# A second Strassen step shared by pairs of text units, and part of the adapter's transposes moved from TensorE to VectorE

## The chip, the cores and the metric

One core of one Trainium2 chip runs the kernel; the other cores are idle. The metric is the device time of one execution in microseconds, as the median of several runs. TensorE is called PE below, its weight loads PEld, VectorE DVE, ScalarE ACT, GpSimd POOL and SyncE SP.

## What is computed

Cross-attention with an adapter, for x of 2 x 2048 x 640 and a context of 2 x 128 x 384, all in float32, with 8 heads of 80:

```python
query = hidden_states @ Wq
hs = _mha(query, enc @ Wk, enc @ Wv)            # 124 text tokens
ca_q1 = einsum('btc,th->bch', ca, Wq_ca)        # 4 adapter tokens -> 384 rows
ca_hs1 = _mha(ca_q1[:, indices], residual, residual)
ca_hs2 = _mha(ca_hs1 @ Wq, ca @ Wk_ca, ca @ Wv_ca)
out = (hs + ca_hs2) @ Wout + b_out + residual
```

`indices` picks 2048 rows out of 384, so the adapter has 384 distinct rows per batch.

## The kernel before

**Work.** The 4096 rows of x are 16 *text units* m of 256 rows (two tiles i of 128). For each, the kernel makes queries (PSUM tiles `pq`), scores (`sc`), a softmax on ACT, DVE and POOL, sends the probabilities through HBM to turn them (`kept`, back as `pT`), multiplies them with the values (`ph`) into the hidden tile `hs`, and multiplies that with Wout (`po`). Beside it runs the *adapter* of each batch b: a first pass of scores (`s1`), whose row maxima DVE takes (`mx`), a second pass (`s2`) whose exponentials ACT takes (`ea`), and a contraction with the rows of y (`acc`). Its row maxima are spread into a tile `mt`, turned by PE transposes into `pm`, subtracted from the operand `ca0` and split into the pair of operands `cop` (`halves_of`, one ACT cast and one DVE instruction over 2 x 384 columns). The result `acc` is copied to `accs`, turned by three PE transposes into `pt_acc`, divided (`prod`), and leads to the 384 adapter rows (`second`). POOL gathers those rows onto each output tile by an indirect DMA (`add_second`) before the tile is stored.

**The product with Wout** (`text_out_fast`, L2392). hs (256 x 640) times Wout (640 x 640) goes by one Strassen step on the first 512 of K: seven products of 128 rows, 256 of K and 320 columns instead of eight, and the last 128 of K, the *fifth*, is multiplied plainly. The sums s1 to s4 of hs are made by DVE or POOL, those of Wout once (`wout_sums`). The seven products stand in four *chains* (L2438), each in one PSUM bank:

```python
            (((a[0][0], w[0][0], None), one_h, ((0, 0),)), ((s2, t2, None), [("hs", m, "s2")], ((1, 0),)),
             ((s1, t1, None), [("hs", m, "s1")], ((0, 1),)), ((None, None, (1, 1)), end_h, ((1, 1),))),
            (((s3, t3, None), [("hs", m, "s3")], ((1, 1),)), ((a[1][1], t4, (1, 0)), both_h + end_h, ((1, 0),))),
            (((a[0][1], w[1][0], (0, 0)), both_h + end_h, ((0, 0),)),),
            (((s4, w[1][1], (0, 1)), [("hs", m, "s4")] + end_h, ((0, 1),)),),
```

Each step is a product added onto what the bank holds; the pair at its end is the quarter (i, u) of the output rows to which DVE then adds the bank (`add`). The next step of the chain waits for that add. One product is written by `by_columns` (L402): four matmuls, one for each 32 columns of the weights, which run side by side in the array; each float32 matmul is two instructions in the trace.

**The order.** The kernel is written as tasks that yield operations (`Do`) with what they wait for and what room they need. A table `TURNS` (L80), worked out ahead, gives every operation its place and engine; `run` (L351) issues by it, and `pin` keeps that order. Where an operation may go to several engines, the table says to which. Text units come in the order 0, 4, 2, 1, 5, 13, 6, 7, 15, 3, 12, 9, 14, 10, 11, 8 (unit 15's product with Wout comes last). Helpers record the instructions, so most rows have L396 (`matmul`), L405 (`by_columns`), L410 (`transpose`), L427 (DVE, ACT and POOL) or L447 (DMA).

Of the kernel before, what the change touches and what calls it, by code (L numbers as in the profile page):

```python
# [8 lines left out]
F32 = mybir.dt.float32  # L9
# [5 lines left out]
P = 128  # L15
# [50 lines left out]
class Desk:  # L66
# [2525 lines left out]
```

## Time and profile before

| | |
|---|---|
| median of 3 runs | 573.56 us (573.53 to 573.89) |
| the profiled execution | 572.92 us |
| its span | 570.9 us |
| PE, PEld busy | 563.0 us, 309.6 us |
| DVE, ACT, POOL busy | 394.5 us, 287.1 us, 160.1 us |
| DMA | 113.21 MB, mean 198 GB/s |
| granted clock of PE | 1.000 |

A row of the timeline or of a group names the line of the helper, the engine, the operation, and the tiles written and read; `128*32 128x320` is a matmul that uses 128 rows and 32 columns of the array and streams 320 columns. Behind the bar stand the busy time of the group in us, the mean of one in ns, and the idle time of the engine just before with what ended it. An arrow in a waits row goes from the engine that waited to the one that released it.

### The profile page before, as it was taken

What the parts mean: (1) busy time and instruction counts of PE and PEld (TensorE: products, weight loads), DVE (VectorE), ACT (ScalarE), POOL (GpSimd) and SP (SyncE); (2) the same over time, 40 slices, a digit from 0 to 9 for tenths busy, and PEclk for the clock granted to TensorE, in tenths of its full rate; (3) what the DMA queues carried; (4) which work ended last, traced back from release to release, by engine and by line L of the source; (5) the groups of instructions that cost most, each with busy time, mean ns of one, the idle gap of its engine ahead of it and who ended that gap; (6) DMA issues with size and microseconds to landing.
All of it is one profiled execution on the core that took longest, in us unless ns stands there. A gap on an engine that the chain in (4) does not pass through costs nothing.

```text
span 570.9 us, 18875 instructions
## 1 busy us (share of the span) xinstructions
PE 563.0 (99%) x8069; PEld 309.6 (54%) x8069; DVE 394.5 (69%) x659; ACT 287.1 (50%) x806; POOL 160.1 (28%) x213
## 2 busy tenths in 40 slices
PE   8999999999999999999999999999999999999997
PEld 8885335455555455466554554555555554455553
DVE  4366999999998577458999999998332213544443
ACT  2021355645566899899885754534554664100000
POOL 9102041114440731100004350531203053045152
PEclk9999999999999999999999999999999999999999
DMA  8998476965968977446646979987476587788888
GB/s 245 219 239 141 125 160 154 175 179 133 209 214 153 221 177 214 149 123 201 228 153 201 328 187 316 224 241 228 94 248 131 167 185 243 251 217 212 255 182 209
DMA packets 145691, 113.21 MB, mean 198 GB/s; under 512 B 82548, under 2 KB 116980, under 8 KB 145608
## 3 DMA queue, kind: packets, MB, share of 16 engines
q1 hardware_dynamic: 137144, 95.43, 59.9%
q0 software_dynamic: 5632, 10.69, 11.6%
q10 hardware_dynamic: 2832, 5.90, 3.0%
q8 instruction: 63, 1.03, 0.8%
q14 instruction: 20, 0.16, 0.1%
HBM read 71.60 MB, written 40.39 MB: 196 GB/s over the span
## 4 chain that ended last, share of the span: by engine, by line
PE 93%; ACT 3%; DVE 3%; DMA 1%; issue 0%; SPq 0%; ACTq 0%
PE po L405 28%; PE pq L405 24%; PE sc L396 8%; PE acc L396 7%; PE ph L396 7%; PE s L396 7%; PE pq L396 4%; PE pyz L396 2%; ACT ea L427 2%; PE pv L396 1%; DVE mx L427 1%; PE pk L396 1%; DMA xz<-in_x_dram 1%; ACT p L427 1%; PE pt_wq L410 1%; PE pw L396 0%
## 5 line engine op out<-in xcount | busy, mean ns | idle before, releaser
L427 ACT ACTIVATE p<-sc,m 128x124 f32<-128x124 f32 x256 | 90.4, 382 | 43.0 <-DVE m L427 38.0
L427 DVE TENSOR_REDUCE mx<-s 128x4 f32<-128x2048 f32 x48 | 109.0, 2270 | 1.9 <-PE s L396 1.9
L427 ACT ACTIVATE ea<-s 128x2048 f32<-128x2048 f32 x48 | 90.5, 1886 | 30.9 <-PE s L396 30.5
L405 PE MATMUL po<-wout_sums,hs 128*32 128x320 f32 x1024 | 78.4, 434 | 0.1
L405 PE MATMUL po<-wout_sb,hs 128*32 128x320 f32 x928 | 72.3, 433 | 0.0
L427 POOL TENSOR_TENSOR p<-p,r 128x992 f32<-128x992 f32 x17 | 31.4, 1849 | 130.9 <-DVE r L427 130.9
L405 PE MATMUL pq<-xt,wq_sb 128*32 128x256 f32 (+1 forms) x928 | 66.4, 418 | 0.0
L427 DVE TENSOR_TENSOR last_rows<-last_rows,po 128x320 f32<-128x320 f32 x60 | 28.0, 480 | 44.0 <-PE po L405 43.8
L427 ACT ACTIVATION_READ_ACCUMULATOR p<-sc,m 128x1 f32 x256 | 57.2, 223 | 0.0
L427 DVE TENSOR_TENSOR x_more<-x_more,po 128x320 f32<-128x320 f32 x68 | 32.3, 480 | 34.2 <-PE po L405 33.7
L405 PEld LDWEIGHTS po<-wout_sums,hs 128*32 128x32 f32 x1024 | 33.4, 110 | 32.7 <-issue 2.7
L427 DVE TENSOR_REDUCE m<-sc 128x4 f32<-128x496 f32 x64 | 40.7, 661 | 14.1 <-PE sc L396 14.0
L396 PE MATMUL acc<-ea,y_sb 128*32 128x384 f32 (+2 forms) x768 | 50.2, 382 | 0.2 <-ACT ea L427 0.2
L396 PE MATMUL ph<-pT,vpad 128*32 128x256 f32 x768 | 47.7, 381 | 0.0
L405 PEld LDWEIGHTS po<-wout_sb,hs 128*32 128x32 f32 x928 | 30.1, 110 | 28.3 <-issue 1.6
L2351 POOL DMA_INDIRECT x_more<-o,query x17 | 26.6, 1564 | 65.2 <-DVE x_more L427 31.1
L405 PEld LDWEIGHTS pq<-xt,wq_sb 128*32 128x32 f32 x928 | 27.7, 110 | 28.0 <-issue 13.5
L427 ACT COPY hs<-ph 128x512 f32<-128x512 f32 (+1 forms) x25 | 13.4, 552 | 57.7 <-PE ph L396 57.7
L427 DVE STREAM_TRANSPOSE eb<-p 128x1024 f32<-128x1024 f32 x32 | 39.4, 1232 | 1.2 <-POOL p L427 1.1
L396 PEld LDWEIGHTS sc<-kmain,q 64*128 64x128 f32 x512 | 31.8, 187 | 12.6 <-issue 5.8
L427 POOL TENSOR_TENSOR hs<-hs 128x256 f32<-128x256 f32 x31 | 28.9, 1020 | 33.7 <-ACT hs L427 25.4
L396 PE MATMUL sc<-kmain,q 64*128 64x124 f32 x512 | 38.0, 285 | 0.0
(219 smaller groups left out, 834.4 us busy)
## 6 DMA issues: line engine op xcount, KB each, us to landing
kept<-eb SPq DMA_DIRECT2D x32, 512.0 KB, 3.5
pT<-kept SPq DMA_DIRECT2D x16, 1024.0 KB, 8.0
landing<-away SPq DMA_DIRECT2D x15, 512.0 KB, 4.8
xi<-in_x_dram SPq DMA_DIRECT2D x56, 128.0 KB, 4.2
x_more<-in_x_dram SPq DMA_DIRECT2D x17, 320.0 KB, 5.0
last_rows<-in_x_dram SPq DMA_DIRECT2D x15, 320.0 KB, 4.8
y<-yt SPq DMA_DIRECT2D x16, 256.0 KB, 3.9
y_sb<-y SPq DMA_DIRECT2D x32, 128.0 KB, 4.0
```

Of the source, the lines that this page charges most:

```text
L396: self.pin(self.nc.tensor.matmul(out, lhsT, rhs, **kw))
L405: self.pin(self.nc.tensor.matmul(out[j : j + 32], lhsT[:, j : j + 32], rhs, **kw))
L410: self.pin(self.nc.tensor.transpose(out, in_, ident))
L427: self.pin(getattr(engine, what)(*args, **kw))
L2351: desk.pin(nc.gpsimd.indirect_dma_start(out=t, out_offset=None, in_=o2_of[b], in_offset=bass.IndirectOffsetOnAxis(ap=query[:, st : st + 1] ...
```

## The change

**Pairs.** Five pairs of text units, (6, 7), (3, 12), (9, 14), (10, 11) and (8, 15), share a second Strassen step. Of the seven products of a unit three, a01 x w10, s4 x w11 and a11 x t4, have weights that both units of a pair use. Stacked, the two units' operands make a product of 256 rows, 256 of K and 320 columns, which is done by seven block products of 128 x 128 x 160 instead of eight (`joint`, PSUM tiles `pi`). The fifths of these three are done in halves of 160 columns beside them. What the inner step needs are sums of Wout quarters, made once (`take_inner`, in the rooms of the softmax tiles `p` and a new `inner_w`), and eight sums per pair (`inner_x0` and others, two buffers), on DVE or POOL. Chain 1 of a paired unit keeps only s3 x t3, which is now added to two quarters. The last unit's s3 x t3 is cut into two halves of columns, and its stores for tile 0 into pieces of 160 columns.

**The adapter.** Of the maxima, half 0 is still turned on the PE; half 1 is turned by 16 DVE transposes of 32 partitions by 3 x 32 (`turned_blocks`), as is `accs` of batch 1, half 0. Each half of `cop` is split on its own, and the scores of half 0 no longer wait for half 1.

**The order.** `turns` puts the pairs behind units 0, 4, 2, 1, 5 and 13, `TURNS` is worked out anew, and the set of first transposes of Wq waits only for its rows.

On the PE, the products of unit 7 that this change moves into the pair, before (`po_7_2` is a01 x w10, `po_7_3` is s4 x w11; `s2` and `acc` are the adapter's):

```order
L405 MATMUL po_7_2_6012<-wout_sb_100,hs_2_5064 32x320 x8
L405 MATMUL po_7_2_6012<-wout_sb_100,wout_sums_4129 32x320 x4
L396 MATMUL s2_1_1_6_6027<-cop_153,zop_1_2_3731 128x384 x4
L396 MATMUL s2_1_1_6_6027<-cop_153,zop_1_2_3731 128x128 x4
L405 MATMUL po_7_3_6037<-wout_sb_100,hs_2_5064 32x320 x8
L405 MATMUL po_7_3_6037<-wout_sb_100,wout_sums_4129 32x320 x4
```

Now the same kind of work on the PE, in pair 1 (units 3 and 12); `pi_1_1_0` is pair 1, product 1, chain 0, and each row of four is one block product:

```order
L434 MATMUL pi_1_1_0_6495<-wout_sb_100,hs_1_4221 32x160 x4
L434 MATMUL pi_1_2_0_6379<-wout_sb_100,hs_0_4133 32x160 x4
L434 MATMUL pi_1_1_2_6507<-wout_sb_100,hs_1_4221 32x160 x4
L434 MATMUL pi_1_1_2_6507<-wout_sb_100,wout_sums_4132 32x160 x4
L434 MATMUL pi_1_2_1_6472<-inner_w_5470,hs_0_4133 32x160 x4
L434 MATMUL pi_1_2_1_6472<-wout_sb_100,hs_0_4133 32x160 x4
L434 MATMUL pi_1_1_0_6495<-p_1_826,inner_x2_5648 32x160 x4
L434 MATMUL pi_1_1_3_6535<-wout_sb_100,inner_x2_5648 32x160 x4
L434 MATMUL pi_1_1_3_6535<-wout_sb_100,wout_sums_4132 32x160 x4
L434 MATMUL pi_1_1_0_6495<-p_1_826,inner_x2_5648 32x160 x4
```

A product of two chunks of 320 columns has become single block products of 160, and between two steps of one chain (the last and the fourth row from the end) stand two others.

On DVE, the adds of pair 0 in the new order (`last_rows` holds the output rows):

```order
L456 TENSOR_TENSOR last_rows_4341<-last_rows_4341,pi_0_2_0_5742 128x160
L456 TENSOR_TENSOR last_rows_4341<-last_rows_4341,pi_0_0_1_5770 128x160
L456 TENSOR_TENSOR last_rows_4341<-last_rows_4341,pi_0_2_2_5776 128x160
L456 TENSOR_TENSOR last_rows_4341<-last_rows_4341,pi_0_2_0_5742 128x160
L456 TENSOR_TENSOR last_rows_4341<-last_rows_4341,pi_0_0_2_5802 128x160
L456 TENSOR_TENSOR last_rows_4341<-last_rows_4341,pi_0_0_1_5770 128x160
```

Before, unit 7's two products above had one add each; every block step has one now, and DVE takes them in this order.

On the PE around the maxima of batch 1, before:

```order
L405 MATMUL po_13_0_5181<-wout_sums_4129,hs_2_5064 32x320 x8
L410 MATMUL pm_1_0_5227<-ident_69,mt_1_5190 128x128 x3
L410 MATMUL pm_1_1_5234<-ident_69,mt_1_5190 128x128 x3
L405 MATMUL po_1_0_5197<-wout_sums_4129,hs_0_4130 32x320 x8
L405 MATMUL po_13_0_5181<-wout_sums_4129,hs_2_5064 32x320 x8
L405 MATMUL po_1_0_5197<-wout_sums_4129,hs_0_4130 32x320 x8
L396 MATMUL s2_1_0_0_5270<-cop_153,zop_1_0_3210 128x384 x4
```

And now:

```order
L434 MATMUL po_1_0_None_5189<-wout_sb_100,hs_0_4133 32x320 x8
L439 MATMUL pm_1_5203<-ident_69,mt_1_5168 128x128 x3
L434 MATMUL po_13_0_None_5173<-wout_sums_4132,hs_2_5049 32x320 x8
L434 MATMUL po_1_0_None_5189<-wout_sums_4132,hs_0_4133 32x320 x8
L425 MATMUL s2_1_0_0_5229<-cop_153,zop_1_0_3220 128x384 x4
```

Three of the six transposes are gone, and the first scores of the second pass stand one po step earlier.

The diff, cut to its core:

```diff
     TURNS = {
-        ".1": [1025], ".2": [44, 59, 60, 84, 96, 108, 114, 120, 126, 132, 150, 174, 198, 210, 234, 1002], ".3":
...
+    def turned_blocks(to, t, after):
+        for i in range(4):
+            def turn(i=i):
+                for g in range(4):
+                    desk.v_transpose(to[G * g : G * (g + 1), :, i], t[G * i : G * (i + 1), :, g])
+            yield Do("DVE", turn, after if i == 0 else None, rank=0)
...
-        yield from halves_of(cop, less, "c", frees=[(eas, at)], marks=[("cop", b)], rank=0)
+        yield from halves_of(cop[:, 0], less[:, 0], "c", marks=[("cop", b, 0)], rank=0)
+        yield Fork(other_half(b, less, mt, at, spread_at), 0)
...
-                op = yield Do("PE", scores, [("cop", b)], needs=[(quad, 1), (eas, 1)], mode=(32, P))
+                op = yield Do("PE", scores, [("cop", b, j)], needs=[(quad, 1), (eas, 1)], mode=(32, P))
...
+        if (b, j) == (1, 0):
+            frees = [(eas, i)]
+            yield from turned_blocks(
...
+        if m in pair_of_unit:
+            chains = (chains[0], (((s3, t3, None), [("hs", m, "s3")], ((1, 1), (1, 0))),))
...
+    PAIRED = ((6, 7), (3, 12), (9, 14), (10, 11), (8, 15))
...
+        for p in range(3):
+            name, a, s = ("m", inner, middle) if p == 1 else (
+                "e", [[outer[r][k][:, p // 2] for k in range(2)] for r in range(2)], ends[:, :, p // 2]
+            )
...
+            steps_of = (
+                (([(a[0][0], w[0][0])], [], (0, 0)), ([(s2, t2)], x(1), (1, 0)), ([(s1, t1)], x(0), (0, 1)),
+                 ([fifth(1, 1)], ends_h, (1, 1))),
+                (([(s3, t3)], x(2), (1, 1)), ([(a[1][1], t4), fifth(1, 0)], ends_h, (1, 0))),
+                (([(a[0][1], w[1][0]), fifth(0, 0)], ends_h, (0, 0)),),
+                (([(s4, w[1][1]), fifth(0, 1)], x(3) + ends_h, (0, 1)),),
+            )
+            for c, steps in enumerate(steps_of):
+                yield Fork(inner_chain(n, pair, p, c, steps, (of4 if p == 1 else []) + ends_h + rows_in, rank), rank)
...
+                    to = bank(s[0], f"pi_{n}_{p}_{c}") if s else po
+                for j, (l, w) in enumerate(pairs):
+                    by_columns(
+                        to[:, : HALF // 2], l, w, start=(k == 0 and j == 0), stop=(j == len(pairs) - 1),
+                        skip_group_check=True,
+                    )
...
+                t = xr_of[pair[r]][i][0][:, u * HALF + v * HALF // 2 : u * HALF + (v + 1) * HALF // 2]
+                desk.b_tensor_tensor(t, t, po[:, : HALF // 2], ALU.add)
...
+    turns = (0, 4, 2, 1, 5, 13, *[m for pair in PAIRED for m in pair])
```

More of the change, by code (lines that the diff above doesn't have):

```diff
@@ L1073, in wq_turned @@
     def wq_turned():
-        yield Do("DVE", lambda: columns(wq_sb, wq4), [("wq", c) for c in range(5)], marks=["wq4"])
+        yield Fork(one(Do("DVE", lambda: columns(wq_sb, wq4), [("wq", c) for c in range(5)], marks=["wq4"])), 2)
         for i in range(NCH):
@@ L1967, in adapter, with other_half @@
         yield Fork(second(b), 0)
+    def other_half(b, less, mt, at, spread_at):
+        yield from turned_blocks(
+            less[:, 1].rearrange("p (a i k) -> p a i k", a=NCC, i=4),
+            mt[:, :, 1].rearrange("p a (g k) -> p a g k", g=4), [spread_at],
+        )
+        yield Do("DVE", lambda: desk.v_tensor_tensor(less[:, 1, :], ca0, less[:, 1, :], ALU.add), rank=0)
+        yield from halves_of(cop[:, 1], less[:, 1], "c", frees=[(eas, at)], marks=[("cop", b, 1), ("cop", b)], rank=0)
+        if b + 1 < B:
+            yield Fork(adapter(b + 1), 0)
     e_of = {}
@@ L2026, in divide @@
             desk.spent += 0.16
[L2028 removed]
+        yield Do("DVE", divide, frees=frees, marks=[("prod", b, j)], rank=0)
     def second(b):
@@ L2457, in product @@
                         by_columns(
-                            to[:, :HALF], l, r, start=(k == 0 and c == 0), stop=(c == len(pairs) - 1),
+                            to[:, cols], l, r[:, cols], start=(k == 0 and c == 0), stop=(c == len(pairs) - 1),
                             skip_group_check=True,
@@ L2497, with inner_of_w @@
     fast_of = {}
-    def stored_half(m, i, u, ends):
+    PAIRED = ((6, 7), (3, 12), (9, 14), (10, 11), (8, 15))
+    pair_of_unit = {m: (n, r) for n, pair in enumerate(PAIRED) for r, m in enumerate(pair)}
+    inner_w, inner_x, xjs = [], [], Room(0)
+    OF_HS = {0: (0, 0), 1: (0, 1), 2: (1, 0)}
+    def inner_of_w(p):
+        if p == 2:
+            w = wsum[3]
+        else:
+            w = wout_sb[:, 2:4, p * HALF : (p + 1) * HALF]
+        return [[w[:, k, n * HALF // 2 : (n + 1) * HALF // 2] for n in range(2)] for k in range(2)]
@@ new lines, in inner_chain, with product, add @@
+    def inner_chain(n, pair, p, c, steps, ready, rank):
+        po, s, at = None, None, []
+        for k, (pairs, after, (r, v)) in enumerate(steps):
+            def product(s=None, k=k, pairs=pairs):
+                to = bank(s[0], f"pi_{n}_{p}_{c}") if s else po
[3 more added lines that the diff above has]
+                        skip_group_check=True,
+                    )
+                return to
+            op = yield Do(
+                "PE", product, after + at + ready, needs=[(banks, 1)] if k == 0 else [], mode=(P, 32), rank=rank
+            )
+            if k == 0:
+                po, s = op.value, op.slots[0][0]
+            end = k == len(steps) - 1
+            if end:
+                desk.event(("inner", n, p, c)).t = op.at.t
+            i, u = OF_HS[p]
+            def add(r=r, v=v, po=po):
+                t = xr_of[pair[r]][i][0][:, u * HALF + v * HALF // 2 : u * HALF + (v + 1) * HALF // 2]
+                desk.b_tensor_tensor(t, t, po[:, : HALF // 2], ALU.add)
+            op = yield Do(
+                "DVE", add, [op.at], frees=[(banks, s)] if end else [], marks=[("isum", n, p, r, v, c)], rank=1
+            )
+            at = [op.at]
@@ L2501, in stored_half, with inner_sums @@
+    def inner_sums(m, i, u):
+        n, r = pair_of_unit[m]
+        for p in range(3):
+            if OF_HS[p] == (i, u):
+                at = {(0, 0): (0, 2), (1, 0): (0, 1), (0, 1): (0, 3), (1, 1): (0, 1)}
+                return [("isum", n, p, r, v, c) for v in range(2) for c in at[r, v]]
+        return []
+    def stored_half(m, i, u, v, ends):
         b, st = tiles(m)[i]
         cols = slice(u * HALF, (u + 1) * HALF)
+        if v is not None:
+            cols = slice((2 * u + v) * HALF // 2, (2 * u + v + 1) * HALF // 2)
```

176 lines of the change are left out of this document (129 added, 47 removed), and 440 rows, old and new, of the table TURNS.

## The prediction

> **What bounds the kernel now.** I read the page first: busy shares, slices, chain.
>
> ```profile
> PE 563.0 (99%) x8069; PEld 309.6 (54%) x8069; DVE 394.5 (69%) x659; ACT 287.1 (50%) x806; POOL 160.1 (28%) x213
> ...
> PE   8999999999999999999999999999999999999997
> ...
> DVE  4366999999998577458999999998332213544443
> ...
> PE 93%; ACT 3%; DVE 3%; DMA 1%; issue 0%; SPq 0%; ACTq 0%
> ```
>
> PE works in every slice but the first and the last, and 93% of the chain that ended last is PE. A busy PE need not be one that does useful work at its peak, so I then read what made it wait.
>
> ```profile
> PE s L396 <- DVE mx L427: 1.1, 2, 0.7
> PE s L396 <- ACT ea L427: 0.6, 3, 0.2
> ```
>
> Behind the start-up these are almost all: 1.7 us. So the time is the PE's own issue time. What the change takes off that queue comes off the end, one for one, unless a new wait gives it back; work for DVE and POOL is free as long as it arrives in time. The profiled run took 572.92 us, of which 570.9 are the span; the median of the runs shown is 573.56, 0.64 us more, and I add that at the end.
>
> **The change, part by part.** *Narrower products.* A product here is four column-tile matmuls of two passes each, so eight instructions, which start in groups of four. The price of a group is read where runs of one tile shape follow each other: from one start to the next, divided by the groups.
>
> ```profile
> 509.07 1.26 PE L405 MATMUL po<-wout_sums,hs 128*32 128x320 f32 x16
> ...
> 513.38 0.72 PE L405 MATMUL po<-wout_sb,wout_sums 128*32 128x320 f32 x8
> ...
> 185.36 1.05 PE L405 MATMUL pq<-xt,wq_sb 128*32 128x256 f32 x16
> 186.22 1.91 PE L405 MATMUL pq<-x_sums,wq_sb 128*32 128x256 f32 x32
> ...
> 52.89 1.00 PE L396 MATMUL pvca<-w_vca,caT 128*32 128x160 f32 x24
> 53.70 1.90 PE L405 MATMUL pq<-xt,wq_sb 128*32 128x512 f32 x16
> ```
>
> 320 columns: 4.31 us from the first row to the last of four runs of 16, sixteen groups, 0.269 each. 256 columns: 0.86 for four, 0.215. 160 columns: 0.81 for six, 0.135. The price is proportional to the width, with next to nothing fixed, so halving the width halves it. In the order of the program 368 matmuls of 320 columns go: 5 pairs x 2 units x 3 products x (2 chunks of K and the fifth) x 4 tiles = 360, and 8 of the last unit, whose step is cut in two. 676 of 160 columns come: 5 x 3 x (7 block products and 4 fifths) x 4 = 660, and 16 of the last unit. At two passes these are 184 groups less at 0.269 = 49.5 us and 338 groups more at 0.135 = 45.6 us: **3.9 us less**. With each 160 group 0.003 us dearer, about what the rounding of these starts allows, it would be 2.9.
>
> A page speaks against this step. The Trainium skill, "TensorE: Matmul & The Clock Gate", section "Back-to-back issue gap", gives 81 ns for each 128-column matmul in a sustained stream, where streaming alone gives 56, because the weight load takes its share. By that ratio, 1.45, the narrow groups would cost 66 us, and the change would be some 17 us dearer than what it removes. The pvca row disagrees: its 24 weight loads leave no trace in 0.81 us.
>
> *Transposes.* Nine 128x128 transposes leave the PE: half of each pm set and one set of pt_acc.
>
> ```profile
> 179.05 0.64 PE L396 MATMUL sc<-krest,rests 64*128 64x124 f32 x8
> 179.63 0.55 PE L410 MATMUL pm<-ident,mt 128*128 128x128 f32 x3
> 180.10 1.27 PE L405 MATMUL pq<-xt,wq_sb 128*32 128x256 f32 x18
> ...
> 391.35 0.88 PE L410 MATMUL pm<-ident,mt 128*128 128x128 f32 x6
> 392.15 2.09 PE L405 MATMUL po<-wout_sums,hs 128*32 128x320 f32 x28
> ...
> 441.49 1.07 PE L396 MATMUL ph<-pT,vpad 128*32 128x256 f32 x16
> 442.50 0.55 PE L410 MATMUL pt_acc<-ident,accs 128*128 128x128 f32 x3
> 442.97 0.50 PE L396 MATMUL s<-cop,zop 32*128 32x384 f32 x8
> ```
>
> A set of three holds the PE 0.47 us (179.63 to 180.10, and 442.50 to 442.97). The queue also drains ahead of it: ph's 16 take 1.01 us, where four 256 groups take 0.86, so some 0.12 goes with a set that stands alone. For batch 0 a whole set goes (0.59), for batch 1 three of six (half of 0.80 less the entry, 0.33), and pt_acc 0.47, since a change of shape to s stays: **1.4 us less**. Other changes of tile shape are as many as before (259 in the old order, 257 in the new).
>
> *What DVE and POOL get.* Nearest rows:
>
> ```profile
> L427 DVE TENSOR_TENSOR x_more<-x_more,po 128x320 f32<-128x320 f32 x68 | 32.3, 480 | 34.2 <-PE po L405 33.7
> ...
> L427 DVE TENSOR_TENSOR hs<-hs 128x256 f32<-128x256 f32 x33 | 16.2, 496 | 5.5 <-POOL hs L427 5.3
> ...
> L427 DVE STREAM_TRANSPOSE xt<-xi 128x512 f32<-128x512 f32 x35 | 23.2, 683 | 0.1
> ...
> L427 DVE TENSOR_TENSOR prod<-prod 128x144 f32<-128x144 f32 x2 | 0.6, 307 | 0.1
> ...
> L427 POOL TENSOR_TENSOR hs<-hs 128x256 f32<-128x256 f32 x31 | 28.9, 1020 | 33.7 <-ACT hs L427 25.4
> ...
> sum 171.00, PE 166.71 PEld 86.31 DVE 63.83 ACT 53.44 POOL 51.63; mean PE 41.68 PEld 21.58 DVE 15.96 ACT 13.36 POOL 12.91
> ```
>
> The last is the sum of four stretches from 400 us to the end. No row has a 160-column add; between 144 columns (307 ns) and 320 (480) I take 0.31, near the first. 124 such adds are 38 us, 22 of 320 columns less save 10.6. About 25 sums for the inner step, half of 256 columns (496) and half of 128 (about 0.3), are 10. The 48 block transposes of 32x96 have no row; they lie between nearly nothing and the 683 ns of 512 columns, and I take 0.2, so 10 us, two thirds of it in this stretch. Copies and hs sums that DVE takes over are some 5. So DVE goes from 64 to about 113 us of 171: not full, but twice as often in the way. Ahead of 390 us, where its slices read 9, its instructions are the same but for a handful and the 16 transposes of batch 0, and five x_sums have gone to POOL. I cost all this at nothing because the PE has other units' work queued between a step and its add; if that cover is gone, see the first rival.
>
> *The dependent steps.* A chain's next step may only overwrite its bank when DVE has read it. The change turns 10 such waits into 60 (four in each of 15 products).
>
> ```profile
> L396 PE MATMUL pvca<-w_vca,caT 128*32 128x160 f32 x24 | 1.0, 299 | 0.0
> ...
> 307.28 2.27 DVE L427 TENSOR_REDUCE mx<-s 128x4 f32<-128x2048 f32 x1
> ...
> 309.61 0.51 PE L396 MATMUL s<-zop,cop 32*128 32x512 f32 x4 [0.45 <-DVE mx L427]
> ```
>
> DVE ends at 309.55 and the PE starts at 309.61: 0.06 us a hand-over. A 160-column matmul takes 0.30, by pvca's row, so the loop is 0.30 + 0.06 + 0.31 + 0.06 = 0.73 us, of which the PE must fill about 0.70. In the new order the tightest place (pi_1_1_0, in the order shown with the change) has two narrow products between, 4 x 0.135 = 0.54: a wait of 0.16. Most have 0.8 or more. The first-half scores now come after two po steps instead of three, while their chain still runs over DVE, ACT and DVE: a few tenths more. I take **1.2 us more** for all new waits, between 0 (all covered) and 9.6 (each as late as the tightest).
>
> *The end.*
>
> ```profile
> 565.42 1.29 PE L405 MATMUL po<-wout_sb,hs 128*32 128x320 f32 x16
> ...
> 566.23 1.03 DVE L427 TENSOR_TENSOR x_more<-x_more,po 128x320 f32<-128x320 f32 x2 [0.61 <-PE po L405]
> ...
> 565.65 1.97 SPq L447 DMA_DIRECT2D out_dram<-x_more  x2
> 567.71 0.41 SPq L447 DMA_DIRECT2D out_dram<-last_rows  x1
> ```
>
> After the last matmul come an add, the store behind it, and one more store in SP's queue. The last matmul and add become 160 wide, 0.13 and 0.17 us shorter; the stores keep their number of queues: **0.3 us less**.
>
> Sum: 3.9 + 1.4 + 0.3 - 1.2 = 4.4 us off 572.92 gives 568.5, and with the 0.64 of the median **569.2 us**.
>
> **The rivals.** *DVE's queue answers late (slower).* From 415 us on, each of the 60 steps waits for an add that stands in order behind copies of 683 ns, sums of 496 and block transposes. For it: DVE's load nearly doubles there and all 60 chains run through one engine. Against it: 113 of 171 us leave a third free, and the order mostly keeps 0.8 us between. It decides from (3.9 + 1.4 + 0.3) / 60 = 0.093 us a step; at 0.16 each it costs 9.6, and the time is 573.56 - 5.6 + 9.6 = 577.6. The Trainium skill, "TensorEngine Tiling (Array Packing)", section "PSUM Bottleneck", has the same warning: tiling speeds the products, not the reading of PSUM, which may become the limit. Here only 64 us of DVE in 171 say how far it was from that before.
>
> *The narrow groups don't come cheaper.* If the weight load set a floor, 160 columns might cost what 256 do, 0.215: 338 x 0.215 = 72.7 instead of 45.6, and the time would be 569.2 + 27 = 596. For it speaks that the PE's weight loads have no row of their own in a long run at this width; against it the pvca row, and that the three widths lie on one line through nearly zero. The page named above points the same way as this rival.
>
> *The PE's gain is given back at the joints.* Each pair's inner products wait for eight sums, some on POOL at 1.02 us behind gathers; one us a pair eats 5 of the 5.6: about 573, no change. For it: both units of a pair must now be ready together, and the last pair has only units 8 and 11 left as cover. Against it: the trace of before shows POOL idle for 33.7 us ahead of such sums with no PE wait.
>
> *More than that.* No new waits, and the 1.7 us behind mx and ea fall away in the new order: 573.56 - 5.6 - 1.7 = 566.3.
>
> **How the numbers follow.** My forecast, 567.3 to 571.6, gets 0.65; DVE late 0.13; narrow groups dear 0.02; given back 0.10; more 0.10. The range takes in the forecast, most of the better case and the lower half of "given back": 566.3 to 573.0, with under 0.2 outside. A measurement of this kernel can tell about 0.2%, 1.15 us, from no change. Faster by more: 0.65 + 0.10 + 0.02 of the fourth = 0.77; within: 0.08, all from it; slower: 0.13 + 0.02 = 0.15.
>
> **What would show it.** The page after should have PE busy near 557 us and still 99%; PE rows pi with 160 columns in runs at 0.135 us a group; six pm and three pt_acc fewer in all; DVE near 445 us, its last slices at 6 or 7. Wrong would be: PE waits named pi <- DVE of over 5 us in sum (first rival), pi groups above 0.16 (second), or waits of pi for POOL or for inner sums once a pair (third).

## The result, and the profile after

The changed kernel takes **581.21 us** (median of 4 runs, 579.91 to 581.66). The kernel before took 573.65 beside it (573.53 to 573.89), so the ratio is **1.0128** [1.0112, 1.0144]: 7.6 us slower, where 4.4 us faster was predicted. A ratio is given with its 95% interval; it is not always the quotient of the two medians beside it. One execution of e5 below (592.93 us) fell into the chip's slower state and is left out of its figures. The profiled execution took 581.21 us with a span of 579.2, 8.3 more than the 570.9 of before.

The page of the changed kernel (busy time, slices, chain):

```profile
PE 563.0 (97%) x8676; PEld 328.5 (57%) x8676; DVE 441.9 (76%) x846; ACT 278.1 (48%) x780; POOL 178.8 (31%) x237
...
PE   8999999999999999999999999999999999999996
...
DVE  3365999999999876568899999998464645576864
...
PE 59%; DVE 18%; DMA 8%; ACT 5%; issue 4%; SPq 2%; POOL 2%; DVEq 0%; ACTq 0%; POOLq 0%
```

PE is busy for exactly as long as before, 563.0 us, and the span has grown by 8.3: all of the difference is idle PE. PE's slices hardly show it, since 1.4% is lost in a digit of tenths; the chain does. PE had 93% of it and has 59%: the end is now set through DVE, DMA and ACT at many places.

The PE waits of the changed kernel, by who was waited for (us in total, times, longest):

```profile
PE pq L425 <- DMA wq_sb<-in_L_xattn_Wq_dram: 1.4, 2, 0.8
...
PE po_None L434 <- DVE last_rows L456: 0.9, 2, 0.7
PE pk L425 <- DVE wqcaT L456: 0.8, 1, 0.8
PE po L425 <- DVE o L456: 0.7, 1, 0.7
PE pq L434 <- DVE q L456: 0.7, 1, 0.7
PE pq L434 <- DVE wq_sums L456: 0.6, 2, 0.4
PE pi L434 <- DVE inner_x L456: 0.6, 1, 0.6
PE pi L434 <- DVE last_rows L456: 0.6, 1, 0.6
PE s L425 <- ACT ea L456: 0.6, 3, 0.2
```

No row is large. Before, two names held nearly all waits behind the start-up. Here nine hold half a microsecond or more each, on DMA, DVE and ACT, from the loads at the start to the last pairs. Only two name the new products (`pi`).

The same time by stages, of before:

```profile
0.00:50.00 50.00, 48.27 (x333) 41.23 (x341) 25.55 (x98) 8.24 (x18) 19.13 (x92) 1.00 0.96 219
50.00:400.00 350.00, 348.00 (x5138) 182.02 (x5126) 305.14 (x419) 225.38 (x744) 89.31 (x80) 1.00 0.72 195
400.00:572.00 172.00, 166.71 (x2614) 86.31 (x2606) 63.83 (x142) 53.44 (x45) 51.63 (x41) 1.00 0.75 199
```

And after. The columns are the window and its length, then busy time and instructions of PE, PEld, DVE, ACT and POOL, the granted clock, the DMA share and GB/s:

```profile
0.00:50.00 50.00, 46.40 (x311) 40.12 (x312) 23.96 (x95) 7.01 (x15) 18.13 (x80) 1.00 0.89 205
50.00:400.00 350.00, 346.62 (x5096) 182.00 (x5098) 309.50 (x438) 216.99 (x719) 96.87 (x96) 1.00 0.73 193
400.00:580.00 180.00, 169.99 (x3279) 106.35 (x3271) 108.47 (x314) 54.07 (x49) 63.76 (x62) 0.99 0.75 198
```

Two stages that the change hardly touches lose PE time, 1.9 us in the first 50 and 1.4 in the next 350. By 400 us PE has worked 3.3 us less, and the first inner product begins only at 433.6.

Busy time hides the other half. A row of eight `pi` instructions lasts 0.48 us and the next one starts after 0.27 (rows below), so a wait of up to 0.2 us lies inside what counts as busy. I therefore also took the time from start to start of successive matmuls, called the median of each pair of tile shapes (both traces pooled) PE's own time, and all above it waiting:

| us | before | after | difference |
|---|---|---|---|
| PE's own time | 554.9 | 550.6 | -4.3 |
| waiting, 0 to 50 us | 2.9 | 5.0 | +2.1 |
| waiting, 50 to 400 us | 6.4 | 8.5 | +2.1 |
| waiting, 400 us to the last matmul | 0.95 | 8.2 | +7.2 |
| behind the last matmul | 4.15 | 5.45 | +1.3 |

The rows sum to +8.4, where the span grew by 8.3. How the matmuls are put into groups of four moves the rows: another cut gives -3.5 for PE's own time and +1.7, +2.2 and +6.9 for the three stretches. The gain on PE came nearly as predicted, then, if somewhat smaller; what came with it is some three times as large.

**The products themselves.** Runs of inner products in the changed kernel's timeline:

```profile
490.61 0.48 PE L434 MATMUL pi<-wout_sb,wout_sums 128*32 128x160 f32 x8
490.88 0.48 PE L434 MATMUL pi<-inner_w,hs 128*32 128x160 f32 x8
...
491.96 0.48 PE L434 MATMUL pi<-wout_sb,wout_sums 128*32 128x160 f32 x8
```

Eight instructions are two groups of four: 0.27 us for two, 0.135 for one, just the price taken from the row of `pvca`.

**The start.** SP's queue in the changed kernel, and DVE behind it:

```profile
23.90 0.68 SPq L476 DMA_DIRECT2D wout_sb<-in_L_xattn_Wout_dram  x1
24.62 0.60 SPq L476 DMA_DIRECT2D w_k<-in_L_xattn_Wk_dram  x1
...
40.19 0.85 DVE L456 COPY k<-w_k 128x192 f32<-128x192 f32 x2 [1.77 <-DMA w_k<-in_L_xattn_Wk_dram]
40.87 0.18 DVE L456 COPY wqcaT<-pt_wqca 128x20 f32<-128x20 f32 x1
```

The load of Wk is issued at 24.62 us, behind a piece of Wout; before, it was issued at 18.40, and DVE copied from it at 30.64 without a wait. Now DVE waits 1.77 us for it, and `wqcaT`, for which PE waits 0.8, stands behind that copy. ACT issues the second piece of Wq at 4.91 us, where before it did at 1.26; hence the 1.4 us for `wq_sb`. None of these lines is in the diff's functions: the table of the order moved them.

**The block transposes.** DVE and PE about the maxima of batch 1:

```profile
399.75 1.12 DVE L456 STREAM_TRANSPOSE mt<-mt 32x96 f32<-32x96 f32 x4
...
400.90 1.08 DVE L456 TENSOR_TENSOR x_more<-x_more,po_None 128x320 f32<-128x320 f32 x2
...
401.90 0.48 DVE L456 TENSOR_TENSOR last_rows<-last_rows,po_None 128x320 f32<-128x320 f32 x1
...
402.43 1.28 PE L434 MATMUL po_None<-wout_sums,hs 128*32 128x320 f32 x16 [0.72 <-DVE last_rows L456]
402.73 1.11 DVE L456 STREAM_TRANSPOSE mt<-mt 32x96 f32<-32x96 f32 x4
```

PE needs the bank that `last_rows` empties. That add stands in DVE's queue behind two others and behind four block transposes of 1.12 us. These were not urgent: their set of sixteen ends only at 407.27 us, and no PE wait bears the name of what it leads to (`cop`). The wait bears the name of an add, but the price is that of what stands ahead of it.

**The end.** The last stores of the changed kernel:

```profile
573.07 1.89 ACTq L476 DMA_DIRECT2D out_dram<-last_rows  x2
...
573.81 0.32 DVE L456 TENSOR_TENSOR last_rows<-last_rows,pi 128x160 f32<-128x160 f32 x1
575.06 0.41 ACTq L476 DMA_DIRECT2D out_dram<-x_more  x1
```

Before, the last store was issued 0.45 us after the last add had ended (567.26 to 567.71), and the span ended 3.2 us later. Now the last store issued is one of `x_more`, whose gather POOL issued at 567.91. It stands in ACT's queue behind stores of 160 columns of the other tile, goes 0.93 us after the last add (574.13 to 575.06), and the span ends 4.1 us after that.

### The profile page after: what moved, and what is told of

The parts are those of the page before. It is cut to its first block, busy times and chain, and to the rows that moved or that the text cites. A ratio compares the mean times of both kernels' runs of the same rounds, so it can differ in the third digit from the quotient of the medians.

```text
span 579.2 us, 20296 instructions
## 1 busy us (share of the span) xinstructions
PE 563.0 (97%) x8676; PEld 328.5 (57%) x8676; DVE 441.9 (76%) x846; ACT 278.1 (48%) x780; POOL 178.8 (31%) x237
## 4 chain that ended last, share of the span: by engine, by line
PE 59%; DVE 18%; DMA 8%; ACT 5%; issue 4%; SPq 2%; POOL 2%; DVEq 0%; ACTq 0%; POOLq 0%
PE pq L434 15%; PE po_None L434 12%; PE pi L434 7%; DVE mx L456 6%; PE acc L425 5%; PE s L425 5%; PE ph L425 5%; PE sc L425 4%; DMA w_k<-in_L_xattn_Wk_dram 3%; ACT ea L456 2%; DMA kept<-eb 2%; SPq L476 2%; ACT p L456 2%; DVE last_rows L456 1%; DVE eb L456 1%
## 5 line engine op out<-in xcount | busy, mean ns | idle before, releaser
L456 POOL TENSOR_TENSOR p<-p,r 128x992 f32<-128x992 f32 x18 | 33.9, 1881 | 129.4 <-DVE r L456 129.4
L434 PE MATMUL po_None<-wout_sums,hs 128*32 128x320 f32 x848 | 65.0, 434 | 0.8 <-DVE last_rows L456 0.7
L434 PE MATMUL po_None<-wout_sb,hs 128*32 128x320 f32 x576 | 44.9, 434 | 0.2 <-DVE last_rows L456 0.2
L434 PEld LDWEIGHTS pq<-xt,wq_sb 128*32 128x32 f32 x928 | 28.0, 109 | 29.0 <-issue 12.2
L434 PEld LDWEIGHTS po_None<-wout_sums,hs 128*32 128x32 f32 x848 | 27.6, 110 | 25.0 <-issue 2.6
L2408 POOL DMA_INDIRECT last_rows<-o,query x16 | 24.8, 1553 | 49.8 <-DVE last_rows L456 41.4
L456 DVE TENSOR_TENSOR x_more<-x_more,po_None 128x320 f32<-128x320 f32 x58 | 27.4, 479 | 11.1 <-PE po_None L434 10.6
L456 POOL TENSOR_TENSOR hs<-hs 128x256 f32<-128x256 f32 x27 | 23.8, 910 | 38.8 <-DVE hs L456 25.1
L425 PEld LDWEIGHTS ph<-pT,vpad 128*32 128x32 f32 x768 | 24.6, 110 | 18.8 <-issue 3.0
L456 DVE TENSOR_TENSOR last_rows<-last_rows,pi 128x160 f32<-128x160 f32 x76 | 22.9, 318 | 16.1 <-PE pi L434 15.4
```

The costliest lines, as they stand in the source:

```text
L425: self.pin(self.nc.tensor.matmul(out, lhsT, rhs, **kw))
L434: self.pin(self.nc.tensor.matmul(out[j : j + 32], lhsT[:, j : j + 32], rhs, **kw))
L456: self.pin(getattr(engine, what)(*args, **kw))
L2408: desk.pin(nc.gpsimd.indirect_dma_start(out=t, out_offset=None, in_=o2_of[b], in_offset=bass.IndirectOffsetOnAxis(ap=query[:, st : st + 1] ...
```

## The experiments

Theories: **A**, the waits come from the new order and from what was put on DVE's queue, at many places; **B**, the chained steps on a bank are late (the first rival); **C**, narrow products cost PE more than their rows show; **D**, the instructions of the change are dearer in any order. What is not named of an edit is as in the changed kernel. Where an experiment replaces the table of the order, one line of it is shown, and `run` then takes its times without `self.now`.

### The changed kernel once more

> The changed kernel once more, unchanged, beside the next three. Both theories: 581.2 within 1.5 us. If its waits for wq_sb in the first 20 us are other ones than the 1.4 us of the first profile (2.0 stood there in the run with copies for blocks, 0.8 in the run without step adds), the time follows them.

581.3 us (578.37 to 583.97) against 573.08, ratio 1.0137 [1.0092, 1.0181]. The same, with a wider spread than that of the kernel before beside it (572.84 to 573.52). In its trace no PE wait names `wq_sb`, but the time did not follow: the profiled execution took 582.21. In their place stands a wait of 1.4 us for `mx`, which ends at 379.53, and behind it the granted clock falls:

```profile
380.00:385.00 5.00, 5.00 (x55) 2.76 (x56) 4.75 (x6) 1.89 (x11) 1.84 (x1) 0.66 0.88 259
```

At 0.66 these five microseconds lose 1.7 us more. In the first profile of the changed kernel `mx` holds PE for 0.3 us, and the clock is 1.00 up to 560 us. So what the small waits cost differs from one execution to the next.

### e1: six loads given back their places

```diff
-        ".4": [5, 52, 70, 76, 88, 100, 340, 466, 574], ".4.1": [37, 163, 175, 229, 253], ".5": [516, 541, 564, 596,
+        ".4": [5, 52, 70, 76, 88, 100, 340, 394, 412], ".4.1": [37, 67, 175, 229, 253], ".5": [516, 541, 564, 596,
```

> The changed kernel with six weight loads put back to where they stood before in SP's and ACT's queues: the second chunk of Wq ahead of ACT's first copy, Wk_ca and Wk between the loads of x, Wv and the two big loads of Wout behind them. Nothing else moves, all work is done. Theory W (the PE's own work fell as forecast, and the loss is made of waits that the new order brings, 2.1 us of them in the first 50 us: 0.81 and 0.57 for wq_sb, 0.82 behind w_k): these waits go, the matmuls that stand at 50 us come 1.5 to 2.1 us earlier, and the time falls by as much from 581.2, to 579.0 to 579.8. Theory C (the loss comes from the 60 chained steps alone, where DVE's adds are late): what is won at the start is lost again at later waits, 581 as before.

583.38 us (582.49 to 583.66), ratio 1.0174 [1.0144, 1.0203]: missed, not faster. The waits for `wqcaT` are gone and those for `wq_sb` down to 0.46, but another took their place. DVE and PE of this run:

```profile
31.58 1.30 DVE L455 STREAM_TRANSPOSE xt<-xi 128x512 f32<-128x512 f32 x2 [3.96 <-DMA xi<-in_x_dram]
32.81 0.65 DVE L455 COPY q<-pq 128x512 f32<-128x512 f32 x1
```

```profile
PE pt_wq L438 <- DVE q L455: 2.6, 1, 2.6
```

The new order of DVE has the transposes of `xi` ahead of a copy that PE waits for, and with the loads that I moved ahead `xi` lands later. So this queue could not be put back alone; that each queue's order fits the landings that it was made for is how I read it. The wait cost more than its length. Windows of this run, columns as above:

```profile
30.00:35.00 5.00, 2.35 (x11) 1.88 (x10) 2.58 (x7) 0.12 (x1) 0.00 (x0) 0.82 0.96 261
35.00:40.00 5.00, 5.00 (x45) 3.76 (x43) 3.49 (x12) 0.15 (x1) 0.00 (x0) 0.84 1.07 209
```

For ten microseconds about it the granted clock is 0.82 and 0.84. The changed kernel's own waits in the first 50 us, 0.8 at most behind the first matmuls, go with a clock of 1.00 in that window.

### e7: the order of before up to the adapter

The instructions that both kernels share stand, at the start, in the order of before, on every queue:

```diff
-        ".1": [671], ".2": [44, 59, 60, 78, 90, 102, 108, 114, 120, 138, 156, 180, 234, 276, 438, 654], ".3": [500],
+        ".1": [1031], ".2": [50, 65, 66, 90, 102, 114, 120, 126, 132, 138, 156, 180, 204, 216, 240, 1008], ".3":
...
-            self.issue(max(self.ready(op), self.free[engine], self.now), engine, op)
+            self.issue(max(self.ready(op), self.free[engine]), engine, op)
```

> The changed kernel in which everything that stood in the first 50 us of the kernel before is issued in the order of before, on all engines and queues (loads, first queries, transposes of Wq); the rest follows in the order of the changed kernel. All work is done. The loads alone did not do it: with six of them put back, DVE stood behind a load of x in its own new order. Theory W: the 2 us that the first 50 us lost come back, the PE has no wait for wq_sb there, and 579.2 or less comes out (578 to 579.8). Against it: the joint between the two orders at 50 us could cost as much, 581.

578.47 us (576.86 to 579.87), ratio 1.0094 [1.007, 1.0119]. The first window of this run:

```profile
0.00:50.00 50.00, 48.45 (x333) 41.56 (x341) 25.91 (x99) 8.24 (x18) 19.09 (x92) 1.00 0.95 217
```

PE has its 48.3 us of before again, and waiting in this stretch is 2.9 us again. By the ratios this took 1.9 to 2.5 us off (1.0128 or 1.0137 to 1.0094, of 573). The intervals of the ratios touch, but with the window's row the start's part is shown, by an edit that leaves the change itself whole. How much of it reaches the end is less sure: in the two profiles the last matmul ends 3.9 us earlier (569.86 against 573.75), so later waits differ too, and 6.6 us lie behind it where the changed kernel has 5.45.

### e2 and e10: one copy for the block transposes of the maxima

```diff
+                if after:
+                    if i == 0:
+                        desk.v_tensor_copy(to.rearrange("p a i k -> p i a k"), t.rearrange("p a g k -> p g a k"))
+                    return
```

e2 has this in the changed kernel, e10 in e7.

> The changed kernel with 32 of the 48 block transposes left out: in the second half of the maxima of both batches one plain copy of 128x384 stands in place of 16 transposes of 32x96. So the maxima of half 1 are not turned; all the rest is done. A block transpose took 0.28 us (a row of 1.11 us for four), 4.5 us a set of 16, and the copy should take about 0.45. Theory W: at 402 and 404 us the PE waits 0.78 and 0.34 us for adds that stand behind such a set on DVE, and some of the 2.1 us that the stretch from 50 to 400 us lost hangs on the other set: 1 to 3 us less, 578.2 to 580.2. Theory C: these sets are ahead of the pairs or beside them, and the time stays within 0.5 us of 581.2.

> Two earlier runs put together: the changed kernel with the first 50 us in the order of before, and a plain copy in place of 32 of the 48 block transposes (the second halves of the maxima are not turned; all the rest is done). The start alone took the kernel from 581.3 to 578.5, the copies alone to 577.9. Theory W (each loss is a wait in a place of its own): they add up, 581.3 - 2.8 - 3.4 = 575.1, between 574 and 576.5. If the one wait only moves into the other's place: 577.5 or more.

e2: 577.92 us (576.17 to 580.67, 7 runs), ratio 1.0085 [1.006, 1.011]. e10: 576.89 (576.55 to 577.27) against 574.02, ratio 1.0047 [1.0029, 1.0065]. Either way 0.43 to 0.52% go, 2.5 to 3.0 us, and by the ratios the two edits add up; the time itself, 576.89, lies above the 574 to 576.5 expected, beside a kernel before that took 574.02 and not 573.08. The place shown above, now of e10 (there it lies 4 us earlier):

```profile
398.09 1.28 PE L431 MATMUL po_None<-wout_sums,hs 128*32 128x320 f32 x16
```

The wait of 0.72 us ahead of `po_None` is gone, though no add was touched. To take 32 transposes off DVE's queue is worth more than the 0.9 us that the prediction had PE save by them.

### e3: no adds for the chained steps

```diff
-            def add(r=r, v=v, po=po):
+            def add(r=r, v=v, po=po, end=end):
+                if not end:
+                    return
```

> The changed kernel with the 60 adds left out after which a chain of block products goes on: DVE adds only the last bank state of each chain of the five pairs, so the output rows lack sums, and no block step waits for DVE within its chain. Theory C: DVE's late answers at these steps are the loss, of which 7.2 us lie behind 400 us: nearly all of it goes, about 574. Theory W: of the waits behind 400 us only about 2.2 us stand ahead of a chained step (0.41 and 0.23 at 490 and 492, 0.58 at 564, 0.22 at 570 and a few smaller), the rest stands at joints, at the adapter's second softmax and behind block transposes; with 14 us less work DVE also reaches those a little earlier: 577.5 to 579.2.

579.59 us (577.47 to 585.05), ratio 1.0122 [1.0053, 1.0191]. Waiting from 400 us on is 7.8 us, against 8.2. The rows that remain in this run:

```profile
PE po_None L434 <- DVE last_rows L456: 0.9, 2, 0.7
...
PE po L425 <- DVE o L456: 0.7, 1, 0.7
```

B would have had nearly all go, to about 574. The interval is wide (one of four executions took 585.05) and by itself leaves room for some four microseconds; it is the trace that decides. With the 60 adds gone the late waits are nearly as long as before and stand where they stood, so B is at most a small part.

### e11: no inner sums behind the second pair, on e7's order

```diff
+                    if n > 1:
+                        return
```

> The changed kernel with the first 50 us in the order of before, and without the eight sums (inner_x) of each of the last three pairs: their inner products read what the buffers hold, so those three pairs' outputs are wrong by that, and no PE step waits for these sums. 24 of 40 sums are left out, some 8 us of DVE and POOL. The third rival on record (each pair's products wait a microsecond or more for its sums): 3 us less than the 578.5 of the kernel with all sums, 575.5. Theory W: the waits named inner_x were 0.6 and 0.2 us in the profiles, with the little that DVE gets free 0.6 to 1.5 us: 577 to 578.

578.17 us (577.41 to 579.85), ratio 1.0067 [1.0049, 1.0085], 1.5 us under e7 by the ratios, 0.3 by the times alone; the intervals overlap. A gain is likely. The third rival, at a microsecond a pair, would have had three; half of that is the best estimate here, and the interval does not shut out more.

### e4: the kernel before with every product with Wout in two halves

```diff
+                        for v in range(2):
+                            part = slice(v * HALF // 2, (v + 1) * HALF // 2)
+                            by_columns(
+                                to[:, part], l, r[:, part], start=(k == 0 and c == 0),
+                                stop=(c == len(pairs) - 1), skip_group_check=True,
+                            )
```

The second half begins its bank anew, so part of the first half's sum is lost; the instructions and their widths are what counts.

> The kernel before, in which every product with Wout (290 of them) is issued as two of 160 columns instead of one of 320, into the same bank, in the same place of the order: 1160 groups of four narrow matmuls in place of 580 wide ones, no add and no wait more, all work done. Theory W (narrow groups cost their width, 0.135 against 0.269): 1160 x 0.135 - 580 x 0.269 = 0.6 us more, and with the 0.1405 a group that the pairs show with their entries 7 more at most: 573.6 to 580, near 574. Theory N (the second rival on record, 0.215 a group): 1160 x 0.215 - 156 = 93 us more, 667.

590.4 us (587.66 to 592.3), ratio 1.0279 [1.024, 1.0317]: 16 us more, which neither theory had. The waits of this run, and two of its matmul rows:

```profile
PE po L405 <- issue: 11.4, 9, 2.7
...
PE sc L396 <- issue: 0.8, 1, 0.8
```

```profile
405.00 0.46 PE L405 MATMUL po<-wout_sb,hs 128*32 128x160 f32 x8
408.17 0.48 PE L405 MATMUL po<-wout_sb,hs 128*32 128x160 f32 x8 [2.71 <-issue]
```

A group is as cheap as before: own time 557.2 us for 555.7 of the same work in wide groups. But ten times PE stands still, 0.6 to 2.7 us and 12.2 in sum, with no engine and no transfer that it waits for. The instruction queue's line of this run has

```profile
q8 instruction: 81, 1.33, 0.9%
```

packets of 16 KB, where the kernel before has 63. Each of the ten stalls ends 2.2 to 2.75 us after one of these transfers began. Behind 400 us thirteen more PE waits have no releaser, in the profiles of a2, e1, e2, e3, e5, e7, e8, e10 and e11 (0.16 to 2.1 us), and each ends 2.2 to 2.5 us after such a transfer began. So PE seems to have run out of instructions; that is a coincidence in time, every time, and wasn't tried by itself. The Trainium skill, "Runtime: NRT & Kernel Launch", section "Instruction fetch mechanics", says that the next 16 KB block is fetched while the current one is worked off, and that the crossing is mostly hidden. This trace disagrees where narrow groups follow each other everywhere, if these stalls are that crossing: 12.2 us lie open. In the changed kernel (68 packets) the rows show one such stall, of some 0.25 us, at 446. So C holds for e4, by a mechanism that I had not named and that is argued, not shown; at the change's dose it is small in the changed kernel, though not in every order of it (e8).

### e5 and e6: both kernels in an order from durations alone

The table is worked out anew for the changed kernel (e5) and, by the same method, for the kernel before (e6).

```diff
-        ".1": [671], ".2": [44, 59, 60, 78, 90, 102, 108, 114, 120, 138, 156, 180, 234, 276, 438, 654], ".3": [500],
+        ".1": [1031], ".2": [50, 65, 66, 90, 102, 114, 120, 126, 132, 138, 156, 180, 204, 216, 240, 1008], ".3":
```

> The changed kernel with the same instructions in another order: the first 50 us as before the change, behind that the places of the operations (and for some sums and copies the engine) worked out anew with the durations that the traces show, block transposes at 0.28 us among them, and with some slack asked for behind each step. All work is done. Theory W (the loss is made of waits that the order brings, and the PE's own work fell by 4.3 us): most of the 11.5 us of waits go, and it comes to 566 to 571, below the kernel before. Theory D (the loss comes with the instructions themselves, however they are ordered: adds between steps, block transposes, instructions that the PE has to fetch): within 2 us of 581.

> The kernel before, its order worked out anew in the same way behind the first 60 us or so, as a measure of what the new order alone is worth without the change. All work is done. The PE of before waits for 2.6 us in all, so no more than that can come off: 570.5 to 573.6. Theory W: the reordered changed kernel beats this one by 2 to 5 us, since 4.3 us of the PE's work are gone. Theory D: this one is the faster, by 7 us or more.

e5: 582.47 us (582.02 to 585.68), ratio 1.0188 [1.015, 1.0226]. e6: 587.78 (586.68 to 589.52), ratio 1.0266 [1.0242, 1.0289]. Both missed: this order costs the kernel before 14.7 us. The largest wait of e5, and what DVE waited for ahead of it:

```profile
PE po_None L431 <- DVE hs L453: 4.3, 1, 4.3
```

```profile
424.51 0.33 DVE L453 TENSOR_TENSOR inner_w<-wout_sums 128x160 f32<-128x160 f32 x1 [6.19 <-DMA kept<-eb]
```

A transfer landed later than the method thought, and all of DVE's queue stood behind it. Yet with orders made alike, the changed kernel is the faster one, by 4.5 us by the ratios, which is near its gain on PE. That speaks against D, though weakly, since both orders have long waits of their own.

### e8 and e9: the two parts of the change apart

e8 is the kernel before with the pairs alone, e9 with the rest alone (the adapter's blocks and the transposes of Wq forked off), each in an order of its own. Of e8, against the changed kernel:

```diff
-        yield from halves_of(cop[:, 0], less[:, 0], "c", marks=[("cop", b, 0)], rank=0)
-        yield Fork(other_half(b, less, mt, at, spread_at), 0)
+        yield from halves_of(cop, less, "c", frees=[(eas, at)], marks=[("cop", b)], rank=0)
```

Of e9, against the kernel before:

```diff
-        yield from halves_of(cop, less, "c", frees=[(eas, at)], marks=[("cop", b)], rank=0)
+        yield from halves_of(cop[:, 0], less[:, 0], "c", marks=[("cop", b, 0)], rank=0)
+        yield Fork(other_half(b, less, mt, at, spread_at), 0)
```

> The pairs without the rest of the change: the kernel before with the second Strassen step of the five pairs, their sums and adds, and the last unit's halves, but with its own adapter (all six transposes of a batch on the PE) and its own transposes of Wq. The first 398 us stand as in the kernel before, on every engine; behind them stand the operations in the order of the changed kernel, with the places on PE, DVE, ACT and POOL smoothed by the durations of the traces and the order of the transfers kept. All work is done. If the changed kernel's loss sits in the pairs (7.2 us of waits behind 400 us, 1.3 behind the last matmul, 2.9 of the PE's work saved): 578 to 579. Theory W, by which the part of the pairs is smaller (1.1 of the 7.2 stood behind block transposes, and a little slack takes off some of the rest): 573 to 576. If the pairs cost nothing: 570.

> The rest of the change without the pairs: block transposes for half of the maxima and for one accs, halves of cop on their own, transposes of Wq as in the changed kernel, and its order of the first 398 us on every engine; the products with Wout and the order of the units as in the kernel before, their places smoothed as in the run beside this one. All work is done. Theory W: 2.8 us for the first 50 us (what the run with before's start got back), 2.1 for 50 to 400, 1.1 for the block transposes at 402, 1.4 less for the transposes gone from the PE: 573.1 + 4.6 = 577.7 (576 to 579). If the pairs carry the loss: 573 or a little less.

Against 574.3 us, e8 took 580.26 (577.1 to 582.3), ratio 1.0091 [1.0056, 1.0126], and e9 577.65 (574.73 to 580.8, 10 runs), ratio 1.0064 [1.004, 1.0088]. Together 1.55%, near the whole's 1.28 to 1.37%. e9 came out at the time expected, though the longer end shown below was no part of that sum; e8 missed, being dearer than the 573 to 576 of theory W (which is A) and also than the 578 to 579 of a loss that sits in the pairs. The largest waits of e8, then of e9:

```profile
PE pi L429 <- POOL inner_x L451: 2.8, 1, 2.8
PE pi L429 <- issue: 2.6, 2, 2.1
```

```profile
PE pk L394 <- DVE wqcaT L425: 1.8, 1, 1.8
```

e9 has the start's wait for Wk without any pair, and a lower clock about it:

```profile
40.00:45.00 5.00, 3.48 (x8) 2.84 (x9) 1.78 (x6) 1.16 (x4) 0.00 (x0) 0.66 0.60 174
```

From 425 us on the view of the waits has no PE row for it. But 6.7 us lie behind its last matmul, where the kernel before has 4.15, though its products with Wout are those of before. This profile is of one of its slower executions (580.32). e8 has the start of before and its losses late: in its order one inner sum on POOL holds PE for 2.8 us, as the third rival had it, and two stalls of e4's look take 2.6. So neither part pays by itself, and the place of a wait is the order's doing as much as the work's.

## Why the prediction was wrong, point by point

- **Narrower products and transposes: right.** Predicted 3.9 + 1.4 = 5.3 us off PE; PE's own time fell by 4.3 (3.5 by the other cut). A pi group takes 0.135 us as said. The second rival, and the rule of the Trainium skill beside it, are refuted as a price of a group; what narrow groups can cost is the stall of e4, of which the changed kernel's profile shows little.
- **PE busy near 557 and 99%: wrong, and badly chosen.** It stayed at 563.0, since short waits count as busy; the idle 8.3 us were the sign.
- **New waits 1.2 us, between 0 and 9.6: this is the step that failed.** It measured 2.1 + 2.1 + 7.2 = 11.4 us, beyond its upper end. It counted the 60 chained steps and the first scores, and by e3's trace the steps are not where most of the time went. It put at nothing the new places of loads at the start and the urgent adds that stand behind new work in DVE's queue; e7 and e2 show these two.
- **"I cost all this at nothing because the PE has other units' work queued": failed.** The cover was judged by DVE's load in a whole stretch (predicted 113 of 171 us; measured 108 of 180). But a queue is late by what stands directly ahead of the add, and PE has its work in a fixed order (`pin`): while the matmul at 402.43 waited its 0.72 us, nothing of what stood behind it ran, so that was no cover. The block transposes are the tested case. I took 0.2 us each; the rows say:

```profile
L456 DVE STREAM_TRANSPOSE mt<-mt 32x96 f32<-32x96 f32 x32 | 8.6, 269 | 0.5
L456 DVE STREAM_TRANSPOSE accs<-accs 32x96 f32<-32x96 f32 x16 | 4.3, 269 | 0.2
L456 DVE TENSOR_TENSOR last_rows<-last_rows,pi 128x160 f32<-128x160 f32 x76 | 22.9, 318 | 16.1 <-PE pi L434 15.4
```

  Four take 1.12 us, 0.28 each, so the 48 are 13.4 us of DVE's time for nine transposes of PE's. Without the first 32 the end came 2.5 to 3.0 us earlier (e2, e10). The Trainium skill, "VectorE: DVE Perf Modes", section "The TRN2 errata", gives a float32 add of N columns as (N + 151) / 0.96 ns, and says that it measured this at 512 and 2048 columns. An estimate by it for smaller N is 324 ns for 160 columns and 257 for 96, of which 157 are fixed. The trace agrees for the add of 160 (318). A block transpose is no add, and the section does not speak of it, but its 269 lie near the add's figure; the estimate of 0.2 had too little fixed time in it. The add of 160 columns, 0.31, was right.
- **"Ahead of 390 us its instructions are the same but for a handful": true of the work, wrong of the order.** 4.2 us of new waiting lie there. At the start, where transfers land just in time, the new order cost 1.9 to 2.5 us, shown by e7; e1 shows that giving six loads their places back is not enough.
- **The end, 0.3 us less: wrong, 1.3 more.** I kept the number of queues and did not look at which store stands last in which queue. Whether that is the cause stays open: e9 ends as late behind its last matmul (6.7 us) without any of the cut stores.
- **DVE late (first rival): its sign was right, its mechanism not.** The `pi` rows that wait for DVE sum to some 1.4 us (waits above 0.15 us), where 5 were named. **Given back at the joints (third rival):** in part, some 1.5 us by e11 in this order, with the interval said there, and 2.8 at one place in e8's.

What the runs account for, of the 7.3 to 7.6 us: -4.3 own time, +1.9 to 2.5 at the start (e7), +2.5 to 3.0 for the maxima's transposes (e2, e10), some 1.5 for inner sums (e11, not certain), up to about 1 for chained steps (e3, not certain), and 1.3 at the end, read from the trace. These numbers are of different executions, and the waits and the clock vary among those. Some 3 us stay, more if the uncertain two are less: single waits that the trace names and that were not tried apart, for `last_rows` at 433.6, for the copy `o` at 498, for `inner_x` at 538, for `wq_sums` and `q` ahead of 400. Nor is it settled whether some other order would let PE's 4.3 us reach the end. None of the versions run beat the kernel before.

## What to carry to other kernels

In a kernel whose PE is 99% busy by a hand-fitted order, ask of each instruction that is moved to another engine which urgent one will stand right behind it in that queue; the engine's free share over a long stretch does not answer that. Compare the new order with the old where transfers land just in time, too, even if the change does nothing there. And judge PE by the distance of starts: a busy share stays the same while real work leaves and short waits come.

## What the runs showed of the hardware

- Halving the width of all products with Wout, at the same price per column, raised PE's matmul records from 8069 to 10373 and opened ten stalls of up to 2.7 us, each ending 2.2 to 2.75 us after a 16 KB transfer of the instruction queue began.
- A PE wait can bring a lower granted clock behind it, and its length alone does not say whether. Waits of 1.4 us (a2), 1.8 (e9), 2.0 (e2), 2.6 (e1), 2.7 (e4), 2.8 (e8) and 4.3 (e5) have a window of five microseconds at 0.82 or less beside them; stalls of 1.4 and 1.7 us in e4 and of 2.1 in e8 have none below 0.98. Windows of e4, around the stall that ends at 408.17:

```profile
405.00:410.00 5.00, 2.29 (x40) 0.96 (x32) 0.89 (x2) 0.82 (x1) 0.00 (x0) 0.93 0.28 74
410.00:415.00 5.00, 5.00 (x84) 3.45 (x80) 1.22 (x3) 1.75 (x2) 0.00 (x0) 0.72 0.07 26
```

  At 0.72 the five microseconds behind it lose up to 1.4 more. Waits under a microsecond, as in the changed kernel's first profile, left the clock at 1.00.
- The kernel before spread over 572.8 to 575.8 us in all its runs here, the other kernels mostly by 1 to 8 us each (e10 by 0.7). Part of it goes with the clock: the two executions of e9 with a mean granted clock of 1.000 took 574.73 and 576.55 us, the three with 0.996 or less 580.03 to 580.80. That the waits themselves hang on the landings of transfers would fit; it was not tried by itself.
